# Coupled rotations of a hybrid layer: a twisted first layer and elementwise cycles in place of a first layer per cycle

## The chip, the cores and the metric

The kernel runs on one core of one Trainium2 chip. The core has five engines that work side by side, each in its own program order: TensorE (PE in the profile; PEld are its weight loads), VectorE (DVE), ScalarE (ACT), GpSimd (POOL) and SyncE (SP), whose queue issues nearly all DMAs here. The metric is the device time of one launch in microseconds.

## The reference, cut to what matters

`x` is 2 x 2048 tokens of 256 features, all float32. Four residual steps follow each other: a grouped softmax attention ("attention A"), the coupled rotation ("ffn"), a causal linear attention with rotary keys ("attention B"), and the coupled rotation again with the same weights. The change lies in the two rotations. Their input is the layer-normalized `x`:

```python
def _twist(x):
    o_r, o_i, p_r, p_i = jnp.split(x, 4, axis=-1)
    return jnp.concatenate([p_r, -p_i, -o_r, o_i], axis=-1)
gf = _global_net(x.mean(axis=1, keepdims=True), ...)    # one number a batch
out = x
for _ in range(3):
    tf = _coupling_net(out, ...)   # 256 -> 256 -> 128 -> 64 -> 1, gelu between, sigmoid last
    coupling = 0.1 + adaptive_range * (0.7 * gf + 0.3 * tf - 0.5) * 2.0
    out = out + coupling * _twist(out)
```

Each token has one coupling a cycle. Twisting twice gives the negative of the input.

## The kernel before, in words

The tokens `xs` stay in SBUF as 32 tiles of 128 tokens x 256 features; they form NB = 8 blocks of BLK = 512 tokens (four a batch). For matrix work a block is normalized and turned by PE into `zq`, [128 features, 2 halves, 512 tokens]. Attention A fills three quarters of the time and is not touched. Everything after it is in `behind`.

`rotations` builds one rotation as a set of small functions. Its unit is k = 0 to 11: pair of blocks k % 4 (two blocks, e = 0 and 1), cycle k // 4. `first(k, e)` is the first layer of one block (L817: two halves of the result, each two products over 128 features; the profile counts two matmuls for each, 8 a call) and its Gelu on ACT (L818). `second(k)` (L827), `third(k)` (L839, both blocks in one bank) and `fourth(k)` follow. In the first two cycles `fourth` makes the coupling of each token on all 128 partitions (L852, tanh on ACT L857, scaling on DVE L858) and updates `zq` in place: one half on DVE (L861, L863), the other on POOL (L862, L864). In the third cycle `back` takes over: the coupling comes out by tokens from eight tiny products (L891), `turn_back` turns `zq` back to tokens on PE (L875) and DVE adds it to `xs` (L879), then adds the twisted part times the coupling (L912). In the second rotation each half block is then stored (L918).

The order of the work is written out by hand: the calls at the end of `behind` follow one another, and `in_order` binds PE, DVE, ACT and POOL to that order. `rounds(f, n)` gives the steady part of a rotation: on even n the fourth layer of k - 2 (third cycle), the second of k - 1 and a first, on odd n the third of k - 1, the fourth of k - 2 and the other first. All matmul results share a ring of seven PSUM banks (`bank`); tiles of SBUF come from small rings by tag (`take`). `context(b)` is the global net in four steps. `Block` is one block of attention B: `look` and `norm` (statistics, normalization; `norm` also adds a constant to `xs` on POOL, L1017), `turn`, `query`, `key` (`rotated`: products on POOL L1034 and L1037, shuffles on DVE, sums in `rotate` L1047), `values`, `narrow`, `gates`, `keys_by_tokens`, `energies`, `learn`, `output`, `project_out`, `add_out`, and `next_look`, `next_norm`, `next_turn` for the second rotation's input. The loop over blocks runs block j beside the projections of block j + 1; the first rotation ends in the preparation of block 0, and the second one begins inside block 7. `statistics` (L106 to L111) has a power on POOL. L119 is the product of the two normalizing numbers of a token tile.

## Time and profile before

| | |
|---|---|
| time, median of 3 runs | 2101.61 us (2099.9 to 2102.15) |
| profiled execution | span 2096.9 us from first to last instruction; its whole time is not listed beside it |
| attention A | until about 1505 us |
| first rotation, then preparation of block 0 | 1505 to 1692 us |
| attention B, blocks 0 to 7 | 1692 to 1943 us |
| rest of the second rotation | 1943 to 2097 us |
| first layer L817 | 384 matmuls, 176.1 us |
| turning back L875 | 128 matmuls, 15.8 us |
| update on POOL, L862 and L864 | 32 + 32, mean 1769 and 1777 ns |
| scaling on DVE, L858 | 32, mean 1023 ns |

In a row of a group, the line and engine come first, then the tile written and the tiles read with shapes and count, then the busy time, the mean of one and the idle time before them with what ended it. A table of stretches gives, for each stretch, its length, the busy time and count of PE, PEld, DVE, ACT and POOL, then the granted clock of TensorE as a share of full speed, the DMA engines' busy share and GB/s. The chain in order of time names the work that ended last, with start and length. Matmuls overlap, so their mean times add up to more than PE's busy time.

### The profile page before, as it was taken

The page shows a single profiled execution, that of the slowest core. Times are in us where ns is not written, and L with a number is a line of the kernel's source. Part 1 is how long each engine was busy: PE and PEld are TensorE (multiplying, and loading weights), DVE is VectorE, ACT ScalarE, POOL GpSimd, SP SyncE. Part 2 cuts the span into 40 slices and gives each one's busy share as a digit, 9 for nine tenths or more (in the row PEclk, how much of TensorE's full clock was granted, in tenths as well). Part 3 has the DMA queues.
Part 4 walks back from the last instruction along what each step waited for, and adds up shares of the span by engine and source line. Part 5 has one row for each costly group of instructions (what it writes and reads, how often), then busy time and mean ns, then how long its engine had stood idle before and what let it go on. Part 6 is the DMA issues. An engine that isn't in the chain of part 4 may idle for free.

```text
span 2096.9 us, 38755 instructions
## 1 busy us (share of the span) xinstructions
PE 2079.2 (99%) x14158; PEld 1009.5 (48%) x14158; DVE 1699.3 (81%) x3241; ACT 1427.6 (68%) x2787; POOL 355.8 (17%) x352
## 2 busy tenths in 40 slices
PE   9999999999999999999999999999999999999998
PEld 4444444444444444444444444444444567776434
DVE  7899989998998999999899899988134688886336
ACT  4477777777777777777777777778864445554443
POOL 3100010000001000000000000000135355542451
PEclk9999999999999999999999999999999999999999
DMA  6511010110101011010110101100100000000002
GB/s 200 149 45 40 18 38 17 50 30 27 38 18 47 10 47 40 17 48 10 47 39 19 38 19 49 38 20 8 53 1 1 0 2 1 1 2 2 0 0 81
DMA packets 59696, 68.72 MB, mean 33 GB/s; under 512 B 24944, under 2 KB 34032, under 8 KB 59248
## 3 DMA queue, kind: packets, MB, share of 16 engines
q1 hardware_dynamic: 58592, 64.79, 11.2%
q8 instruction: 111, 1.82, 0.3%
q10 hardware_dynamic: 720, 0.92, 0.2%
q14 instruction: 81, 0.66, 0.1%
q0 software_dynamic: 192, 0.52, 0.1%
HBM read 35.78 MB, written 26.21 MB: 30 GB/s over the span
## 4 chain that ended last, share of the span: by engine, by line
PE 96%; DVE 2%; ACT 1%; DMA 1%; issue 0%; POOL 0%; SPq 0%; DVEq 0%; ACTq 0%; POOLq 0%
PE av L632 24%; PE s L376 24%; PE p L650 11%; PE q1f L817 8%; PE p L654 6%; PE q2f L827 4%; PE pe L1126 2%; PE bpo L1152 2%; PE pv L984 1%; PE po L499 1%; PE pq L975 1%; PE pk L975 1%; PE pw L984 1%; PE q3f L839 1%; PE pq L336 1%; DVE mx L380 1%
## 5 line engine op out<-in xcount | busy, mean ns | idle before, releaser
L380 DVE TENSOR_REDUCE mx<-s 128x1 f32<-128x512 f32 x2048 | 1273.8, 683 | 103.6 <-PE s L376 97.7
L658 ACT ACTIVATE e<-p 128x512 f32<-128x512 f32 x2048 | 1057.7, 602 | 306.3 <-PE p L654 299.5
L376 PE MATMUL s<-a_kP,qP 64*128 64x512 f32 x2048 | 707.3, 470 | 4.4 <-DVE mx L380 2.4
L654 PE MATMUL p<-a_m,a_pick 64*128 64x512 f32 x2048 | 578.0, 414 | 0.0
L376 PEld LDWEIGHTS s<-a_kP,qP 64*128 64x128 f32 x2048 | 283.6, 184 | 568.9 <-DVE mx L380 533.3
L632 PE MATMUL av<-e,a_v 128*32 128x512 f32 x4096 | 546.2, 605 | 0.1
L650 PE MATMUL p<-qP,a_kP 64*128 64x512 f32 x2048 | 521.8, 394 | 2.0 <-ACT e L658 2.0
L650 PEld LDWEIGHTS p<-qP,a_kP 64*128 64x128 f32 x2048 | 283.4, 185 | 65.4 <-issue 15.9
L654 PEld LDWEIGHTS p<-a_m,a_pick 64*128 64x128 f32 x2048 | 282.0, 184 | 24.0
L817 PE MATMUL q1f<-zq,wf 128*128 128x512 f32 x384 | 176.1, 601 | 0.0
L632 PEld LDWEIGHTS av<-e,a_v 128*32 128x32 f32 x4096 | 80.9, 108 | 128.1 <-issue 119.1
L398 POOL TENSOR_TENSOR mt<-nm,mt 128x16 f32<-128x16 f32 x31 | 6.9, 222 | 742.9 <-ACT mt L397 742.9
L818 ACT ACTIVATE a1f<-q1f,wf 128x512 f32<-128x512 f32 x96 | 65.8, 687 | 94.5 <-PE q1f L817 91.3
L817 PEld LDWEIGHTS q1f<-zq,wf 128*128 128x128 f32 x384 | 70.2, 190 | 96.9 <-issue 86.2
L1132 DVE TENSOR_TENSOR en<-pe,small 128x512 f32<-128x512 f32 x128 | 79.4, 683 | 11.8 <-PE pe L1126 11.8
L858 DVE TENSOR_SCALAR cf<-cf,f_beta,alphaf 128x512 f32<-128x512 f32 x32 | 32.7, 1023 | 67.6 <-ACT cf L857 67.6
L827 PE MATMUL q2f<-a1f,wf 128*128 128x512 f32 x192 | 87.0, 595 | 0.0
L237 POOL TENSOR_TENSOR ql<-zq,qh 128x512 f32<-128x512 f32 x15 | 19.4, 1292 | 364.5 <-ACT qh L234 364.5
L862 POOL TENSOR_TENSOR tf<-cf,zq 128x512 f32<-128x512 f32 x32 | 56.6, 1769 | 102.3 <-DVE cf L858 101.8
L829 ACT ACTIVATE a2f<-q2f,wf 128x512 f32<-128x512 f32 x48 | 32.7, 686 | 56.2 <-PE q2f L827 56.2
L864 POOL TENSOR_TENSOR zq<-zq,tf 128x512 f32<-128x512 f32 x32 | 56.9, 1777 | 2.5
L491 POOL TENSOR_TENSOR oc<-oc,sums 128x512 f32<-128x512 f32 x16 | 20.6, 1289 | 210.2 <-DMA sums<-dr 126.8
(210 smaller groups left out, 1634.6 us busy)
## 6 DMA issues: line engine op xcount, KB each, us to landing
qP<-dq SPq DMA_DIRECT2D x64, 256.0 KB
dq<-qh SPq DMA_DIRECT2D x62, 128.0 KB
dq<-ql SPq DMA_DIRECT2D x62, 128.0 KB
a_kP<-dk SPq DMA_DIRECT2D x16, 256.0 KB
oc<-avs SPq DMA_DIRECT2D x128, 32.0 KB
sums<-dr SPq DMA_DIRECT2D x128, 32.0 KB
out<-xs SPq DMA_DIRECT2D x16, 256.0 KB
xs<-in_x SPq DMA_DIRECT2D x7, 512.0 KB
```

The lines of the kernel that those rows point to most:

```text
L376: mm(s, qP[r // 2][row, qi * P : (qi + 1) * P], kP[r // 2][row, k0 + kb * BLK : k0 + (kb + 1) * BLK], start=True, stop=True,)
L380: nc.vector.tensor_reduce(mx[:, r, qi : qi + 1, kb], s, AX.X, ALU.max)
L632: mm(av[32 * r : 32 * r + 32, :], vA[:, units[u][0] // BPB * KB + kb, 32 * r : 32 * r + 32], es[r], start=(kb == 0), stop=(kb == KB - 1),)
L650: mm(t[r], kP[r // 2][row, k0 : k0 + P], qP[r // 2][row, :], start=True, stop=False)
L654: mm(t[r], pick[row, :], mrow[r // 2][row, :], start=False, stop=True)
L658: nc.scalar.activation(es[r], t[r], AF.Exp, scale=1.0 / HD**0.5)
L817: mm(q1, w1[:, c, m * P : (m + 1) * P], z[:, c, :], start=(c == 0), stop=(c == 1))
L818: nc.scalar.activation(a1[:, m, :], q1, AF.Gelu, bias=b1[:, m : m + 1])
L827: mm(q2, w2[:, c, :], a1[:, c, :], start=(c == 0), stop=(c == 1))
L862: nc.gpsimd.tensor_tensor(t1, cs, z[:, 0, :], ALU.mult)
L864: nc.gpsimd.tensor_tensor(z[:, 1, :], z[:, 1, :], t1, ALU.subtract)
L1132: nc.vector.tensor_tensor(self.ens[t][w], pes[w].rearrange("p (h n) -> p h n", h=4), const("triu").unsqueeze(1).to_broadcast([P, 4, P]), A ...
```

## The change

With u the first layer of z (without bias) and v the first layer of the twisted z, the first layer after a cycle with coupling c1 is u + c1 v, and that of the twisted result is v - c1 u. So `first` now keeps u (a copy out of PSUM, by DVE, or by ACT in block 7), `twist` makes v with a second set of weights `twisted` and writes it over z in `zq`, and `couple` forms the next cycle's first layer elementwise: in cycle 1 h = u + c v on DVE and v - c u on POOL, in cycle 2 h + c v with one of the two products on POOL. `again` applies bias and Gelu to it out of SBUF. The first layer is made twice per block instead of three times, and `back`, `turn_back` and `turn_ahead` go.

The tokens are now updated from `x` itself: each token's result is a combination of its normalized features and their twist with two numbers from the three couplings. The couplings of cycles 1 and 2 exist along the free axis; one partition's row of each goes to DRAM and comes back by tokens (`rows`, two DMAs a cycle and block and one back a pair, on SP). `ready` and `weigh` (`weights_of`) form the numbers, and `apply` does four token tiles: two scalings of twisted halves (POOL, or ACT in two places) and one step on DVE. The normalizing numbers are kept for all blocks (`scales0`, `scales1`). Pairs are staggered: `period(f, p, aside)` runs pair p through cycle 1, pair p - 1 through cycles 2 and 3, and the update of pair p - 2. In block 0 of attention B the query's and key's first product moves from POOL to DVE.

```diff
-beta = hold.tile([P, 1], F32, name="f_beta")
-nc.vector.tensor_scalar(beta, plain, sign, None, ALU.mult)
+
+twisted = hold.tile([P, 2, D], F32, name="f_twisted")
+for c in range(2):
+    nc.vector.tensor_scalar(twisted[:, c, :], w1[:, 1 - c, :], sign, None, ALU.mult)
+nc.vector.tensor_scalar(twisted[:, 0, :], twisted[:, 0, :], -1.0, None, ALU.mult)
+scales1 = hold.tile([P, 2, NB, 4], F32, name="scales1")
...
+    def activate(k, cycle, e, of, tags=(("qs", "ks"), ("rotq", "rotk"))):
+        a1 = acts[k, e] = take(tags[min(cycle, 2) - 1][e], [P, 2, BLK], f"a1f{n}_{k}_{cycle}_{e}")
         for m in range(2):
+            nc.scalar.activation(a1[:, m, :], of(m), AF.Gelu, bias=b1[:, m : m + 1])
+    def layer(w, k, e, name, between=()):
+        z = blk(zq, 2 * k + e)
+        q = [bank(f"{name}{n}_{k}_{e}_{m}") for m in range(2)]
+        for m in range(2):
+            if m == 1:
+                for step in between:
+                    step()
             for c in range(2):
+                mm(q[m], w[:, c, m * P : (m + 1) * P], z[:, c, :], start=(c == 0), stop=(c == 1))
+        return q
+    def first(k, e, copy=nc.vector.tensor_copy):
+        q = layer(w1, k, e, "q1f")
+        activate(k, 1, e, lambda m: q[m])
+        straight[k, e] = take(("gate", "v")[e], [P, 2, BLK], f"uf{n}_{k}_{e}")
+        for m in range(2):
+            copy(straight[k, e][:, m, :], q[m])
+    def twist(k, e, between=(), copy=nc.scalar.copy):
+        q = layer(twisted, k, e, "q5f", between)
+        for m in range(2):
+            copy(blk(zq, 2 * k + e)[:, m, :], q[m])
+    def second(k, cycle, e):
+        a1 = acts.pop((k, e))
+        q2 = bank(f"q2f{n}_{k}_{cycle}_{e}")
+        for c in range(2):
+            mm(q2, w2[:, c, :], a1[:, c, :], start=(c == 0), stop=(c == 1))
+        narrow[k, e] = take("en", [P, BLK], f"a2f{n}_{k}_{cycle}_{e}")
+        nc.scalar.activation(narrow[k, e], q2, AF.Gelu, bias=b2)
+    def third(k, cycle):
+        q3 = bank(f"q3f{n}_{k}_{cycle}")
         for e in range(2):
+            mm(q3[64 * e : 64 * e + 64, :], w3, narrow.pop((k, e)), start=True, stop=True)
+        narrow[k] = take("en", [P, BLK], f"a3f{n}_{k}_{cycle}")
+        nc.scalar.activation(narrow[k], q3, AF.Gelu, bias=b3)
+    def fourth(k, cycle):
+        a3 = narrow.pop(k)
+        q4 = [bank(f"q4f{n}_{k}_{cycle}_{e}") for e in range(2)]
         for e in range(2):
             row = slice(64 * e, 64 * e + 64)
             mm(q4[e], w4[row, :], a3[row, :], start=True, stop=True)
         for e in range(2):
+            c = turns[k, e] = take("en", [P, BLK], f"cf{n}_{k}_{cycle}_{e}")
+            nc.scalar.activation(c, q4[e], AF.Tanh, bias=hb4, scale=0.5)
+    def couple(k, cycle, e, tags=("kt", "kt2"), own_tags=("rotq", "rotk"), spare=nc.gpsimd):
+        c = turns.pop((k, e))
+        nc.vector.scalar_tensor_tensor(
+            c, c, plain, plains[2 * k // BPB].to_broadcast([P, BLK]), ALU.mult, ALU.add
+        )
+        if (k, 1) not in rows:
+            rows[k, 1] = dram.tile([4, BLK], F32, tag="cr", name=f"cr{n}_{k}")
+        at = 2 * (cycle - 1) + e
+        nc.sync.dma_start(rows[k, 1][at : at + 1, :], c[0:1, :])
+        v = blk(zq, 2 * k + e)
+        if cycle == 1:
+            u, h = straight[k, e], take(tags[e], [P, 2, BLK], f"hf{n}_{k}_{e}")
+            sums[k, e] = h
+            back = [take("qeo", [P, BLK], f"tf{n}_{k}_{e}_{m}") for m in range(2)]
+            for m in range(2):
+                nc.vector.tensor_tensor(h[:, m, :], c, v[:, m, :], ALU.mult)
+                nc.vector.tensor_tensor(h[:, m, :], h[:, m, :], u[:, m, :], ALU.add)
+                spare.tensor_tensor(back[m], c, u[:, m, :], ALU.mult)
+            for m in range(2):
+                spare.tensor_tensor(v[:, m, :], v[:, m, :], back[m], ALU.subtract)
+        else:
+            h = acts[k, e] = take(own_tags[e], [P, 2, BLK], f"a1f{n}_{k}_{cycle}_{e}")
+            u = sums.pop((k, e))
+            spare.tensor_tensor(h[:, 1, :], c, v[:, 1, :], ALU.mult)
+            nc.vector.tensor_tensor(h[:, 0, :], c, v[:, 0, :], ALU.mult)
+            for m in range(2):
+                nc.vector.tensor_tensor(h[:, m, :], h[:, m, :], u[:, m, :], ALU.add)
+        if (cycle, e) == (2, 1):
+            rows[k] = hold.tile([P, 2, 8], F32, name=f"ct{n}_{k}")
+            nc.sync.dma_start(
+                rows[k].rearrange("p c t -> p (c t)"),
+                rows[k, 1].rearrange("c (t p) -> p (c t)", p=P),
+            )
+    def again(k, cycle, e, tags=("rotq", "rotk")):
+        if cycle == 2:
+            activate(k, cycle, e, lambda m: sums[k, e][:, m, :], ((), tags))
+        else:
+            h = acts[k, e]
+            for m in range(2):
+                nc.scalar.activation(h[:, m, :], h[:, m, :], AF.Gelu, bias=b1[:, m : m + 1])
+    def ready(k):
+        c, f = rows.pop(k), take("small", [P, 2, 8], f"ab{n}_{k}")
+        nc.vector.tensor_tensor(f[:, 0, :], c[:, 0, :], c[:, 1, :], ALU.mult)
+        nc.vector.tensor_scalar(f[:, 0, :], f[:, 0, :], -1.0, 1.0, ALU.mult, ALU.add)
+        nc.vector.tensor_tensor(f[:, 1, :], c[:, 0, :], c[:, 1, :], ALU.add)
+        quarter[k] = f
+    def weights_of(k):
+        a3, f = narrow.pop(k), quarter.pop(k)
+        q4 = bank(f"q4f{n}_{k}_3")
         for tile in range(4):
             mm(
                 q4[:, 2 * tile : 2 * tile + 2], a3[:, tile * P : (tile + 1) * P], w4_pair,
                 start=True, stop=True,
             )
+        c, g = (take("small", [P, 2, 8], f"{a}f{n}_{k}") for a in ("c", "g"))
+        nc.scalar.activation(
+            c[:, 0, :].rearrange("p (e t) -> p e t", e=2), q4[:, 0:8].rearrange("p (t e) -> p e t", e=2),
+            AF.Tanh, bias=hb4, scale=0.5,
+        )
+        nc.vector.tensor_scalar(c[:, 0, :], c[:, 0, :], plain, plains[2 * k // BPB], ALU.mult, ALU.add)
+        nc.vector.tensor_tensor(g, f, c[:, 0:1, :].to_broadcast([P, 2, 8]), ALU.mult)
+        nc.vector.tensor_tensor(c[:, 0, :], f[:, 0, :], g[:, 1, :], ALU.subtract)
+        nc.vector.tensor_tensor(c[:, 1, :], f[:, 1, :], g[:, 0, :], ALU.add)
+        sc = scaled[:, :, 2 * k : 2 * k + 2, :].rearrange("p s e t -> p s (e t)")
+        by_rs, by_nb = take("small", [P, 3, 8], f"r{n}_{k}"), take("small", [P, 2, 8], f"n{n}_{k}")
+        nc.vector.tensor_tensor(by_rs[:, 0:2, :], c, sc[:, 0:1, :].to_broadcast([P, 2, 8]), ALU.mult)
+        nc.vector.tensor_tensor(by_nb, c, sc[:, 1:2, :].to_broadcast([P, 2, 8]), ALU.mult)
+        nc.vector.tensor_scalar(by_rs[:, 2, :], by_rs[:, 1, :], -1.0, None, ALU.mult)
+        nc.vector.tensor_scalar(by_rs[:, 0, :], by_rs[:, 0, :], 1.0, None, ALU.add)
+        nc.vector.tensor_tensor(g[:, 0, :], by_nb[:, 0, :], by_nb[:, 1, :], ALU.add)
+        nc.vector.tensor_tensor(g[:, 1, :], by_nb[:, 0, :], by_nb[:, 1, :], ALU.subtract)
+        quarter[k] = by_rs, g
+    def apply(k, e, by_tile=(nc.gpsimd.tensor_scalar,), home=None):
+        by, of = quarter[k]
+        j = 2 * k + e
+        if home is not None:
+            others = take(home, [P, 4, D], f"of{n}_{j}")
+        for t in range(4):
+            i = 4 * e + t
+            x = xs[:, 4 * j + t, :]
+            other = take("swap", [P, D], f"of{n}_{j}_{t}") if home is None else others[:, t, :]
+            x4, o4 = (a.rearrange("p (u f) -> p u f", u=4) for a in (x, other))
+            for m, (to, frm) in enumerate((
+                (slice(0, 4, 3), slice(2, 0, -1)), (slice(1, 3), slice(3, None, -3)),
+            )):
+                by_tile[t % len(by_tile)](
+                    o4[:, to, :], x4[:, frm, :], by[:, 1 + m, i : i + 1], of[:, m, i : i + 1], ALU.mult, ALU.add,
+                )
+            nc.vector.scalar_tensor_tensor(x, x, by[:, 0, i : i + 1], other, ALU.mult, ALU.add)
+            if store and t % 2:
+                s0 = (j % BPB) * BLK + (t - 1) * P
+                nc.sync.dma_start(
+                    out[j // BPB, s0 : s0 + 2 * P, :].rearrange("(t p) d -> p t d", p=P),
+                    tokens(j)[:, t - 1 : t + 1, :],
+                )
+    return context, first, twist, second, third, fourth, couple, again, ready, weights_of, apply
...
-            nc.gpsimd.tensor_tensor(r[:, m, :], a[:, m, :], c, ALU.mult)
+            (nc.gpsimd if j else nc.vector).tensor_tensor(r[:, m, :], a[:, m, :], c, ALU.mult)
...
+def period(f, p, aside, early=False):
+    first, twist, second, third, fourth, couple, again, ready, weigh, apply = f[1:]
+    def beside(n):
+        for step in aside.get(n, ()):
+            step()
+    q, o = p - 1, p - 2
+    if not early:
+        first(p, 0)
+    beside(0)
+    if o >= 0:
+        weigh(o)
+    again(q, 2, 0)
+    if o >= 0:
+        apply(o, 0)
+    beside(1)
+    twist(p, 0)
+    again(q, 2, 1)
+    for e in range(2):
+        second(q, 2, e)
+    beside(2)
+    first(p, 1)
+    if o >= 0:
+        apply(o, 1)
+    beside(3)
+    third(q, 2)
+    twist(p, 1, (step(fourth, q, 2), step(couple, q, 2, 0)))
+    beside(4)
+    second(p, 1, 0)
+    couple(q, 2, 1)
+    again(q, 3, 0)
+    second(p, 1, 1)
+    beside(5)
+    second(q, 3, 0)
+    again(q, 3, 1)
+    third(p, 1)
+    beside(6)
+    second(q, 3, 1)
+    beside(7)
+    fourth(p, 1)
+    couple(p, 1, 0)
+    beside(8)
+    third(q, 3)
+    ready(q)
+    couple(p, 1, 1)
+    beside(9)
...
 # the order of calls in the first rotation after pair 0's cycle 1 (one call a line in the code):
+period(f, 1, {2: (step(turn_next, 6), step(norm, 7)), 6: (step(turn_next, 7),), 7: (step(next, front1),), ...}, True)
+period(f, 2, {5: (step(next, more),), 8: (step(next, more),)})
+period(f, 3, {1: (zero.look,), 4: (step(zero.norm, late),), 6: (zero.turn, one.look)})
+zero.query(); one.norm(work); weigh(2); zero.rotate(); zero.key(); again(3, 2, 0, ...); again(3, 2, 1, ...)
+zero.values(0); second(3, 2, 0); second(3, 2, 1); zero.rotate(); zero.narrow(); third(3, 2); one.turn()
+fourth(3, 2); couple(3, 2, 0, ...); zero.values(1); couple(3, 2, 1, ...); zero.gates(); zero.keys_by_tokens()
+zero.halve(0); again(3, 3, 0); again(3, 3, 1); second(3, 3, 0); zero.ready(0); zero.energies(0)
+second(3, 3, 1); zero.learn(0); third(3, 3); ready(3)
 # in block 0 of attention B: weigh0(3), then apply of pairs 2 and 3 with the scalings on ACT
...
 # after block 7, the second rotation:
+period(f, 1, {0: (x.next_turn,), 3: (step(next, front1),), 4: ..., 6: ..., 8: ...}); period(f, 2, {})
 first(3, 0)
+weigh(1); again(2, 2, 0); apply(1, 0); twist(3, 0); again(2, 2, 1)
 first(3, 1)
+apply(1, 1); second(2, 2, 0); second(2, 2, 1); twist(3, 1, (step(third, 2, 2),)); fourth(2, 2); couple(2, 2, 0)
+second(3, 1, 0); second(3, 1, 1); couple(2, 2, 1); third(3, 1); again(2, 3, 0); again(2, 3, 1); fourth(3, 1)
+couple(3, 1, 0); second(2, 3, 0); second(2, 3, 1); couple(3, 1, 1); third(2, 3); again(3, 2, 0); again(3, 2, 1)
+second(3, 2, 0); ready(2); second(3, 2, 1); weigh(2); third(3, 2); fourth(3, 2); couple(3, 2, 0); couple(3, 2, 1)
+apply(2, 0); again(3, 3, 0); again(3, 3, 1); second(3, 3, 0); second(3, 3, 1); apply(2, 1); third(3, 3)
+ready(3); weigh(3); apply(3, 0, (by_act, nc.gpsimd.tensor_scalar)); apply(3, 1, (by_act, nc.gpsimd.tensor_scalar))
```

## The prediction

> **What bounds the kernel now.** I read the page first (busy shares, slices, chain), then the table of stretches, then the chain in order of time through a rotation, then the timeline of VectorE (DVE) and GpSimd (POOL).
>
> ```profile
> PE 2079.2 (99%) x14158; PEld 1009.5 (48%) x14158; DVE 1699.3 (81%) x3241; ACT 1427.6 (68%) x2787; POOL 355.8 (17%) x352
> PE 96%; DVE 2%; ACT 1%; DMA 1%; issue 0%; POOL 0%; SPq 0%; DVEq 0%; ACTq 0%; POOLq 0%
> ```
> ```profile
> 1740.00:1760.00 20.00, 20.00 (x216) 15.62 (x220) 15.70 (x44) 10.33 (x24) 8.68 (x12) 1.00 0.00 1
> ...
> 2000.00:2020.00 20.00, 20.00 (x53) 7.76 (x52) 7.44 (x9) 9.07 (x14) 11.68 (x7) 1.00 0.00 0
> ```
> ```profile
> 1995.89 3.63 PE q1f L817 x8
> 1999.52 3.43 PE q2f L827 x8
> 2002.95 3.43 PE q1f L817 x8
> 2007.39 1.06 PE q4f L852 x4
> 2008.45 3.63 PE q1f L817 x8
> ```
> The columns of a stretch after its length are PE, weight loads, DVE, ACT, POOL. TensorE (PE) is full in both rotations; in a rotation DVE is idle 63% of the time, in the attention between them (first line) only 22%. One cycle of one pair of blocks takes 12.57 us (1995.89 to 2008.45), all PE: two first layers (3.63 + 3.43), a second (3.43), a third (1.02, left out of the merged chain) and a fourth (1.06). The third cycle replaces the fourth layer's 1.06 by eight tiny matmuls (0.97) and 16 transposes (1.81). A pair costs 2 x 12.57 + 14.3 = 39.5 us.
>
> What the change will meet stands in the timeline (start, us, engine, line):
> ```profile
> 1997.36 0.69 DVE L861 TENSOR_TENSOR tf<-cf,zq 128x512 f32<-128x512 f32 x1
> ...
> 1999.83 1.50 DVE L858 TENSOR_SCALAR cf<-cf,f_beta,alphaf 128x512 f32<-128x512 f32 x1
> ```
> ```profile
> 1997.40 1.78 POOL L862 TENSOR_TENSOR tf<-cf,zq 128x512 f32<-128x512 f32 x1 [4.96 <-DVE cf L858]
> 1999.26 1.78 POOL L864 TENSOR_TENSOR zq<-zq,tf 128x512 f32<-128x512 f32 x1
> ```
> ```profile
> L1047 DVE TENSOR_TENSOR rotq<-rotq,swapqs x12: 682/685/1762, 1700.7 to 1859.9; 128x512 f32<-128x512 f32 x12
> ```
> POOL's 128x512 product takes 1.78 us when it starts 0.04 us behind a DVE product with both inputs in SBUF, 1.27 elsewhere (L1034): it stood 0.5 us until DVE was done. The DVE scaling at 1999.83, issued behind POOL's, takes 1.50 where 0.55 is usual. L1047 has a median of 685 ns and a maximum of 1762. So such instructions of the two engines exclude each other; their times add.
>
> **What is removed.** L817 has 384 matmuls, 8 a call, 48 calls; after it are 32 (a straight and a twisted call per block): 16 x 3.53 = 56.5 us. The transposes: 8 x 1.81 = 14.5. Together 71 us of PE, all on the path. A pair needs 4 x 3.53 + 3 x 3.43 + 3 x 1.02 + 2 x 1.06 + 0.97 = 30.6 us.
>
> **What is added, per pair.** DVE: four copies of 0.6 from PSUM; 18 products and sums of 128x512 with two SBUF inputs at 0.60 back to back (10 in cycle 1, 8 in cycle 2) = 10.8; eight `apply` steps of 128x256 (0.42 by L1157, 0.38 back to back) = 3.0; 13 tiny operations, 2.0. POOL: eight products and differences in cycle 1, two in cycle 2, at 1.24 back to back = 12.4; 16 scalings of 128x128 with two scalars, a form not in the trace: between 0.20 (a 4-element product, L119) and 0.73 (128x256 product, L1017), and I take 0.35, nearer the tiny one for half the elements and one tensor input = 5.6. ACT: four copies of 0.59 from PSUM, and the Gelus as before; some 20 us, no bound. The two-SBUF-input work and POOL's add to 10.8 + 3.0 + 12.4 + 5.6 = 31.8 us, over PE's 30.6: a second bound at once, before any latency.
>
> Whether the `apply` forms exclude each other too, no row shows. The Trainium skill ("SBUF — State Buffer", Who interferes with whom) says that a VectorE instruction with two SBUF inputs and a GpSimd instruction reading SBUF hold one port pair in turn, the later fully blocked. That would cover them; if they overlapped, the sum would be some 3 us a pair lower.
>
> **One period** (`period`, t = 0 where PE begins the fourth layer of a pair's cycle 1). From 1594.63 (q4f) to 1596.65 (L858) DVE gets the coupling after 2.0 us. `couple` of both blocks: ten DVE steps of 0.6, 0.4 for `ready`, and since each next DVE step finds a POOL product already waiting, seven of 1.24 between: 15.1, so the last sum stands at 17.1. Gelu 0.7, last half of the second layer 0.9: 18.7. PE had work for 10.7 of that (fourth 1.06, third 1.02, next pair's first 3.43, 0.97, twist 3.43, and the other second layer until it too waits). Then first, third, half a twist: the next fourth at 24.9, its coupling at 27.0. DVE meanwhile: copies 1.2, tiny 1.6, `apply` 8 x 0.35 + 4 x 0.38 = 4.3, copies 1.2, second `apply` 2.9 (POOL is ahead): 28.3. `couple` of cycle 2: eight steps and two POOL products, 7.3: 35.6; Gelu and half a second layer: **37.2 us**, against 30.6 of PE and 39.5 before. 6.7 of the 8.9 gained come back as waits.
>
> **The sum**, waits of PE that today has none:
> - opening to the first fourth layer (six first-layer calls, four turns and small work in the same stretch): 2.5.
> - rotation 0: period 1 carries two turns and the context, 3.7; period 2, 5.3 (the linear weights' DVE work hides in its slack); period 3 has `zero.look` (DVE 1.9) ahead of `apply`, `zero.norm` (four POOL sums of 0.73 between the two cycle-2 products) and the 1.1 of the offset: 43 us, 11.5 of it waiting.
> - pair 3's cycles 2 and 3 beside block 0's query, key and values (28 us of PE): `couple` to 17.1, then DVE and POOL in order through the query's rotation, `weigh`, `rotate` and the key's before `couple` starts at 32, ends at 39.4, and third layer and energies end at 42.7: 14.5.
> - block 0 of the attention takes 16 `apply` steps (6 us DVE, 32 ACT scalings) into a stretch with 22% of DVE free: 3 (0 to 6).
> - rotation 1: period 1, 4; period 2, 6.7.
> - the end, from pair 2's fourth layer, with no other work to fill: pair 2's coupling at 27.6, pair 3's at 37.0, its last sum 51.8, its cycle 2 coupling 58.5, sums 65.8, last third layer 69.2, `apply` of pair 2 until 73.2, `ready` and `weigh` 75.3, eight `apply` steps 80, output 3 more (2093.8 to 2096.9 today): 83 us for 51 of work that today follows without waits: 31.6. The coupling rows go out by SP and return in 4-byte pieces; a round trip's rows: 1.6 us (rs from ds) a hop, the mean packet 64 engine-ns (11.2% of 16 spans over 58592) times 2048 over 16 queues = 8.2. Between 3 and 11 us against 10.5 free: hidden.
>
> Waits 82.8, less 71: plus 11.8. Last, the clock:
> ```profile
> 2085.00:2090.00 5.00, 3.05 (x21) 1.92 (x19) 3.80 (x14) 1.64 (x3) 0.00 (x0) 0.94 0.20 69
> 2090.00:2097.00 7.00, 0.00 (x0) 0.00 (x0) 3.80 (x15) 0.00 (x0) 0.00 (x0) 0.50 0.45 152
> ```
> The granted clock (third column from the right) is 0.50 once PE stands idle, and PE would stand 4 to 8 us at a time at the end. Halved matmuls there cost between nothing and the 6 us of PE work on that chain; I take half, 3. Rows cannot price it in the periods. The skill ("TensorE: Matmul & The Clock Gate", Part 1) wants 3.4 us idle for the fall and 3.4 us busy for the return; each of five stalls would then cost up to 1.7 us more, and the sum would be about 8 higher, partly behind DVE.
>
> Span 2096.9 + 11.8 + 3 = 2111.7; the median shown, 2101.6, lies 4.7 above the span (start and stop around it, the own time of that execution not being listed), so **2116 us**. Its own bounds: POOL's scaling at 0.20 or 0.73 (-10, +15 where it is on the path, some five periods' halves and the end), block 0 and clock (3 each way): 2100 to 2134.
>
> **Rivals.**
> A, faster: POOL's products fall into DVE's gaps instead of between its steps, so the last sum of cycle 1 stands by 11 us, before PE runs out of work. It decides at that point: then periods are 31 to 32 and waits fall by some 5 in five periods and 10 more at handover and end, 2116 - 35 = 2081. For it: in today's cycle POOL is only 58% busy and DVE 37%. Against: the 1.78 and 1.50 rows.
> B, much slower: POOL's scaling near its upper bound and the clock falling in every stall: 2116 + 15 + 10 = 2141.
> C: the returned coupling rows land after 10.5 us and `ready` holds DVE, with both blocks' `couple` queued behind it: plus 2 in each of six places, 2128.
> That the matmuls do not go is no case: the order of instructions has 9501 PE rows for 9565, and 32 first-layer calls.
>
> **How the numbers follow.** Forecast 0.50, A 0.31, B 0.12, C 0.07. The range must reach A and most of B: 2078 to 2140; the forecast's own is 2100 to 2134. Some 0.2% (4 us) can be told from no change: 2097.4 to 2105.8 is the same. Faster: A and little else, 0.32; same: the low edge of the forecast, 0.08; slower 0.60.
>
> **What would show it.** PE under 90% in the rotations with waits on a1 (ACT, behind DVE's sums) before the second layer; DVE sums in `couple` of 1.8 us beside POOL's 1.24; periods of 37 us; a tail of some 80 us behind pair 2. Wrong if the 128x512 sums have a median of 0.69 with POOL at 1.27, periods come to 31, or POOL's scaling takes over 0.5.

## The result, and the profile after

The changed kernel takes 2137.5 us (median of 4 runs, 2135.8 to 2139.8) against 2100.8 for the kernel before on the same chip: a ratio of 1.0178 (95% interval 1.0164 to 1.0193). It is slower by 36.8 us; the forecast was slower by 14.4. The profiled execution spans 2136.9 us, 40.0 more than the one before. (Each run takes 1.8 us longer than its span, so the span before, 2096.9, belongs to a run of some 2098.7, a short one; that is why 40.0 is more than 36.8.) The page's busy times, then the chain's shares:

```profile
PE 2047.9 (96%) x13902; PEld 981.0 (46%) x13902; DVE 1795.8 (84%) x3279; ACT 1461.3 (68%) x2865; POOL 420.5 (20%) x452
...
PE 84%; DVE 10%; ACT 2%; POOL 2%; issue 1%; DMA 1%; SPq 0%; POOLq 0%; DVEq 0%; ACTq 0%
```

PE's idle time (span less busy) is 89.0 us where it was 17.7, and DVE's part of the chain has gone from 2% to 10%. PE's busy time fell by only 31.3 us, although 71 us of its work were to go; some of the products that stay take longer (a matmul of the second layer, L847, 688 ns instead of 595), in part because of the clock, as will be shown. The stretches (PE, weight loads, DVE, ACT, POOL, then granted clock) in attention B, in the second rotation and at the end:

```profile
1740.00:1760.00 20.00, 20.00 (x183) 13.26 (x182) 17.22 (x46) 9.36 (x22) 11.75 (x12) 1.00 0.01 2
2015.00:2035.00 20.00, 16.02 (x41) 6.75 (x40) 17.15 (x31) 8.22 (x14) 17.48 (x19) 0.91 0.04 13
2100.00:2120.00 20.00, 14.26 (x30) 4.98 (x28) 10.24 (x22) 6.84 (x11) 7.92 (x10) 0.60 0.08 11
```

In the rotation PE is no longer full. DVE and POOL are busy 17 of 20 us each, and much of that is waiting, as the groups show (busy, mean ns of one):

```profile
L888 POOL TENSOR_TENSOR tf<-cf,uf 128x512 f32<-128x512 f32 x32 | 54.5, 1722 | 44.2 <-DVE cf L873 43.5 <-ACT zq L841 0.7
...
L887 DVE TENSOR_TENSOR hf<-hf,uf 128x512 f32<-128x512 f32 x32 | 52.4, 1637 | 1.1
...
L886 DVE TENSOR_TENSOR hf<-cf,zq 128x512 f32<-128x512 f32 x32 | 39.1, 1222 | 0.6
```

A sum of 0.6 us (0.69 alone) takes 1.64, and POOL's product 1.72 instead of 1.27: each stands until the other engine's step is done (e1 and e2 test this). One period of the chain in order of time:

```profile
1577.37 1.11 PE q4f L865 x4
...
1588.52 1.64 DVE hf L887
1590.15 1.69 DVE hf L886
...
1591.87 1.64 DVE hf L887
...
1594.30 2.08 PE q2f L847 x2
...
1614.91 1.11 PE q4f L865 x4
```

The last sum of cycle 1 ends 16.1 us behind the start of the fourth layer (1577.4 to 1593.5; forecast 17.1), then PE's second layer follows, at half its speed (2.08 us for two matmuls that take 1.12), and the next fourth layer starts 37.5 us behind the first.

The table cuts the profiled executions at matmuls that both rotations and all versions have. P1 to P3: from the fourth layer (cycle 1) of pair 0 to those of pairs 1, 2 and 3 in the first rotation. H: from there to the query of block 1. B: to the second rotation's first layer. S: to the fourth layer of pair 1. P5: to that of pair 2. E: to the end. All in us; the start of P1 differs by up to 3 us between executions (1537.6 to 1540.9), so stretches are compared rather than spans.

| version | P1 | P2 | P3 | H | B | S | P5 | E | median (us) |
|---|---|---|---|---|---|---|---|---|---|
| changed kernel | 39.4 | 37.5 | 42.5 | 46.6 | 229.0 | 77.8 | 37.5 | 88.7 | 2137.5 |
| e1 couple on DVE | 35.9 | 34.8 | 43.4 | 42.4 | 228.8 | 74.0 | 35.9 | 76.8 | 2111.8 |
| e2 POOL writes only | 29.9 | 33.2 | 36.4 | 39.5 | 228.9 | 68.9 | 31.4 | 73.8 | 2084.2 |
| e3 apply on DVE | 38.7 | 38.2 | 42.2 | 45.9 | 228.8 | 77.7 | 38.3 | 88.6 | 2142.1 |
| e4 PE kept busy | 37.1 | 37.6 | 42.5 | 47.0 | 229.1 | 75.9 | 37.3 | 88.7 | 2139.6 |
| e5 second buffer | 39.6 | 37.6 | 42.5 | 46.6 | 227.0 | 78.9 | 37.7 | 88.7 | 2138.4 |
| e6 keys later | 38.7 | 37.6 | 43.0 | 43.3 | 227.6 | 77.8 | 37.5 | 88.7 | 2135.8 |
| e7 order at two joints | 39.5 | 37.6 | 42.5 | 46.5 | 229.1 | 70.7 | 37.7 | 86.3 | 2130.6 |
| e8 DVE, deferred | 29.9 | 33.8 | 42.8 | 42.6 | 228.9 | 68.9 | 35.1 | 72.5 | 2095.9 |
| e9 updates spread | 39.8 | 37.7 | 42.5 | 46.6 | 225.7 | 77.9 | 37.5 | 88.6 | 2136.1 |
| e10 e8 and joints | 29.9 | 33.8 | 41.8 | 40.7 | 225.7 | 67.9 | 33.8 | 75.7 | 2088.9 |
| e11 and mixed scalings | 29.9 | 43.4 | 43.7 | 39.4 | 225.7 | 67.9 | 43.3 | 81.6 | 2115.3 |
| e12 and earlier look | 29.9 | 42.3 | 45.8 | 39.5 | 225.7 | 67.9 | 43.3 | 81.6 | 2116.1 |
| e13 updates at block ends | 39.9 | 37.7 | 42.5 | 46.6 | 221.6 | 78.2 | 37.7 | 88.7 | 2132.0 |
| e14 the best | 29.9 | 33.8 | 41.8 | 40.7 | 221.6 | 67.9 | 33.8 | 72.6 | 2082.2 |

The kernel before has only some of these cuts: B is 219.9 there; from its first first layer (1504.9) to block 1's query it takes 187.2 us (changed kernel 199.1), from the second rotation's first layer to the end 185.0 (204.0). So of the 40.0, 11.9 are lost in the first rotation with the handover, 9.1 in attention B and 19.0 in the second rotation.

### The profile page after: what moved, and what is told of

Read it like the earlier page. It is cut to its first block, busy times and chain, and to the rows that moved or that the text cites. A ratio compares the mean times of both kernels' runs of the same rounds, so it can differ in the third digit from the quotient of the medians.

```text
span 2136.9 us, 38472 instructions
## 1 busy us (share of the span) xinstructions
PE 2047.9 (96%) x13902; PEld 981.0 (46%) x13902; DVE 1795.8 (84%) x3279; ACT 1461.3 (68%) x2865; POOL 420.5 (20%) x452
## 4 chain that ended last, share of the span: by engine, by line
PE 84%; DVE 10%; ACT 2%; POOL 2%; issue 1%; DMA 1%; SPq 0%; POOLq 0%; DVEq 0%; ACTq 0%
PE av L633 23%; PE s L378 23%; PE p L651 11%; PE p L655 6%; DVE hf L887 2%; PE q2f L847 2%; DVE hf L886 2%; PE pe L1178 2%; PE q1f L826 2%; PE bpo L1204 1%; PE q5f L826 1%; PE po L500 1%; PE pw L1036 1%; PE pv L1036 1%; PE pq L1027 1%; PE pk L1027 1%
## 5 line engine op out<-in xcount | busy, mean ns | idle before, releaser
L847 PE MATMUL q2f<-a1f,wf 128*128 128x512 f32 x192 | 107.6, 688 | 47.2 <-ACT a1f L815 32.7
L847 PEld LDWEIGHTS q2f<-a1f,wf 128*128 128x128 f32 x192 | 36.0, 207 | 107.4 <-ACT a1f L815 51.6
L888 POOL TENSOR_TENSOR tf<-cf,uf 128x512 f32<-128x512 f32 x32 | 54.5, 1722 | 44.2 <-DVE cf L873 43.5
L826 PE MATMUL q1f<-zq,wf 128*128 128x512 f32 x128 | 62.2, 631 | 0.0
L826 PE MATMUL q5f<-zq,f_twisted 128*128 128x512 f32 x128 | 60.4, 607 | 0.0
L849 ACT ACTIVATE a2f<-q2f,wf 128x512 f32<-128x512 f32 x48 | 32.7, 684 | 37.1 <-PE q2f L847 30.8
L967 DVE SCALAR_TENSOR_TENSOR xs<-xs,r,of 128x256 f32<-128x256 f32 x64 | 32.9, 530 | 26.2 <-POOL of L964 22.5
```

Of the source, the lines that this page charges most:

```text
L826: mm(q[m], w[:, c, m * P : (m + 1) * P], z[:, c, :], start=(c == 0), stop=(c == 1))
L847: mm(q2, w2[:, c, :], a1[:, c, :], start=(c == 0), stop=(c == 1))
L888: spare.tensor_tensor(back[m], c, u[:, m, :], ALU.mult)
```

## The experiments

**e1: couple on DVE alone.**

```diff
-def couple(..., own_tags=("rotq", "rotk"), spare=nc.gpsimd):
+def couple(..., own_tags=("rotq", "rotk"), spare=nc.vector):
```

> Edit: couple's products and differences on POOL move to DVE (spare=nc.vector); all else as in the changed kernel. Theory (two-input DVE and POOL instructions take turns): the sums of cycle 1 (hf L887) fall from 1.64 to 0.69 us, the last sum of a pair's cycle 1 stands 11 to 12 us after its fourth layer instead of 16, periods of 33 to 34 us instead of 37.5, and the time falls from 2137 to about 2112 (2104 to 2120). Rival 1 (DVE's load and its chain of steps set the period): DVE gets 20 more steps of 0.6 us in two pairs, 6 us a pair, and the time rises to 2150 or more. Rival 2 (the lowered clock after waits is most of the loss): 2125 to 2135.

2111.8 us, ratio to before 1.0047 (1.0032 to 1.0062). Ten products and differences a pair more on DVE, and it is 26 us faster. The sum is back at its own length:

```profile
L887 DVE TENSOR_TENSOR hf<-hf,uf 128x512 f32<-128x512 f32 x32 | 22.1, 692 | 1.1
```

**e2: POOL writes where it read.** Left out: the difference v - c u of cycle 1; POOL writes zeros instead, twenty times a pair.

```diff
     nc.vector.tensor_tensor(h[:, m, :], h[:, m, :], u[:, m, :], ALU.add)
-    spare.tensor_tensor(back[m], c, u[:, m, :], ALU.mult)
-for m in range(2):
-    spare.tensor_tensor(v[:, m, :], v[:, m, :], back[m], ALU.subtract)
+    for _ in range(5):
+        spare.memset(back[m], 0.0)
```

> Leaves out part of the computation: v - c u of cycle 1 isn't made; POOL's four instructions there are replaced by ten memsets (write only) of the same scratch tiles, about 5 us of POOL a block as before. Theory as the trace shows it (turns are taken only where POOL reads SBUF too, as in the products): DVE's sums at 0.69 beside a busy POOL, last sum 8 to 9 us after the fourth layer, periods of 31 to 33, time about 2105 (2095 to 2115). If any POOL work holds DVE up, its sums stay over 1 us and the time stays above 2125. Rival 1 (DVE's own chain): no change, 2130 to 2140.

2084.2 us, ratio 0.9913 (0.9896 to 0.993), lower than expected. POOL stays as busy beside the sums (20 memsets of 0.53 us a pair for eight products and differences, forecast at 1.24), but reads nothing:

```profile
L889 POOL MEMSET tf<- 128x512 f32 x160 | 83.7, 531 | 7.4
L887 DVE TENSOR_TENSOR hf<-hf,uf 128x512 f32<-128x512 f32 x32 | 22.1, 692 | 1.1
```

So it is POOL's reading of SBUF beside DVE's two inputs that costs, not POOL being busy. The rule of the Trainium skill that the prediction cites ("SBUF — State Buffer", Who interferes with whom) names just this condition, and these rows agree with it: 692 ns beside writes, 1637 beside reads. The rest of e2's gain over e1 (P1 29.9 to 35.9) is, by its size, DVE's eight steps of the difference, which nobody makes here; e8, where they come later, has the same P1.

**e3: apply's scalings on DVE**, the rival that POOL's 0.54 us each were the missing cost.

```diff
-def apply(k, e, by_tile=(nc.gpsimd.tensor_scalar,), home=None):
+def apply(k, e, by_tile=(nc.vector.tensor_scalar,), home=None):
```

> Edit: apply's scalings of 128x128 on DVE instead of POOL (except in block 0 and for the last pair, where ACT takes them or half of them). Theory: in a period DVE is free for cycle 2 only 0.3 us after the coupling arrives, so a period loses less than 0.5 us; the end, where 16 POOL scalings of 0.52 stand on the chain (9.6 us), gets some 4 us shorter: 2131 (2126 to 2136). Rival (POOL's scaling at 0.54 instead of the 0.35 that was predicted is the missing cost): 8 tiles x 0.35 us a pair come back in every period, 2115 to 2122.

2142.1 us, ratio 1.019 (1.0175 to 1.0205): a little slower, above both ranges. Two scalings on DVE take 2 x 0.34 and then the step; from POOL DVE waits about as long for them. P2 is 38.2 against 37.5. The 4 us expected at the end did not come either: E is 88.6 against 88.7, because DVE now has the scalings and the steps one after the other, 1.04 us a tile where POOL and DVE together took 1.11.

**e4: PE kept busy in its wait.** Five extra products with constants (ten rows of the profile) ahead of one second layer a period.

```diff
+for _ in range(warm):
+    mm(q2, w2[:, 0, :], twisted.rearrange("p c d -> p (c d)"), start=True, stop=True)
```

> Adds five matmuls of a constant (128x512, into the bank that the second layer overwrites) where PE waits for block 1's cycle-2 Gelu in each period: nothing of the result changes. Rival 2 (clock): granted clock back to 1.00 in those stretches, the second layer after the wait 1.1 instead of 2.1 us and the next first layer 3.6 instead of 4.2: 1.5 us in each of five periods, 2130 (2126 to 2133). Theory (DVE's turns set the period, DVE is free only 0.3 us after the coupling): most of that is lost in DVE's wait, under 0.5 us a period, 2134 to 2138.

2139.6 us, ratio 1.0175 (1.016 to 1.019): no gain. In the first periods of the two rotations the stretches P1 and S are 2 us shorter each, in the steady ones nothing moves (37.6, 37.3), although the first layer behind the wait runs at full speed again (3.60 us instead of 4.20). But in P2 the extra products also end 0.9 us behind the Gelu that PE waits for, which uses up what the clock gives back: the next fourth layer (cycle 2) starts 26.0 us behind the first, against 25.9. So there e4 by itself does not price the clock. The rows of the changed kernel do:

```profile
1604.38 1.27 ACT L868 ACTIVATE cf<-q4f,f_hb 128x512 f32<-128x512 f32 x2 [2.24 <-PE q4f L865]
1604.90 0.48 DVE L967 SCALAR_TENSOR_TENSOR xs<-xs,r,of 128x256 f32<-128x256 f32 x1 [0.35 <-POOL of L964]
1605.31 0.75 DVE L873 SCALAR_TENSOR_TENSOR cf<-cf,f_plain,plainf 128x512 f32<-128x512 f32 x1
```

The first of the two tanh ends at 1605.07, and DVE is done with its `apply` steps at 1605.31, so an earlier coupling could have been taken up only 0.2 us sooner.

**e5: a second buffer for the updates in block 0.**

```diff
-apply0(3, 0, home="zt")
+apply0(3, 0, home="kt2")
```

> In block 0 of attention B the update of pair 3's first block puts its scaled halves into another tile (kt2) than the update before it (zt); all else is as in the changed kernel. In the changed kernel ACT's scalings for that block wait 2.74 us for DVE to read the tile, the gate's tanh stands behind them in ACT's order, and PE waits 3.26 us for it, with eight products at half clock behind (3.78 instead of 1.99). Theory (the loss in block 0 is ACT's order): the tanh starts 2.5 to 2.9 us earlier, PE's wait falls under 1 us, the time falls by 3 to 5 us, to some 2133. Rival (it is DVE's load by the added steps, as the prediction had it): DVE's steps are the same and in the same order, so nothing over 1 us changes: 2137.

2138.4 us: no gain in time, and 2.0 us in B, about half of what was expected. PE's wait for ACT, first row (changed kernel), gives way to one for DVE, second row (e5):

```profile
1727.64 2.07 PE L1178 MATMUL pe<-qeo,rotk 32*128 32x256 f32 x10 [3.26 <-ACT gate L1140]
```
```profile
1733.19 1.11 PE L1048 MATMUL pt<-small,rotk 128*128 128x128 f32 x4 [2.54 <-DVE og L1209]
```

Neither theory holds: both engines are late here, one just behind the other.

**e6: keys turned later at the handover.**

```diff
 zero.gates()
-zero.keys_by_tokens()
 zero.halve(0)
+zero.ready(0)
+zero.energies(0)
 again(3, 3, 0)
 again(3, 3, 1)
 second(3, 3, 0)
-zero.ready(0)
-zero.energies(0)
 second(3, 3, 1)
+zero.keys_by_tokens()
 zero.learn(0)
```

> Between the rotations the keys of block 0 are turned to tokens (keys_by_tokens) behind pair 3's third cycle instead of ahead of it, and block 0's first energies ahead of it. In the changed kernel ACT's copies of the turned keys wait 7.04 us for the tile that still holds pair 3's sums, until DVE has made the last of them, and the Gelus of pair 3's third cycle stand behind them in ACT's order. Theory: the Gelus start by about 1691 instead of 1693.96, PE's wait of 4.5 us falls to about 2, the query of block 1 starts 2 to 4 us earlier (1703.9 now): time 2134, between 2133 and 2136. Rival (DVE's sums alone set that end, the second block's at 1695.7): the second block's Gelu and everything behind it stay where they are, less than 1 us: 2137.

2135.8 us, within the expected range; H falls from 46.6 to 43.3. In the changed kernel the copy of the turned keys stands on ACT ahead of pair 3's Gelus:

```profile
1692.19 1.07 ACT L1147 COPY kt<-pt 128x512 f32<-128x512 f32 x2 [7.04 <-DVE a1f L897]
...
1693.96 2.55 ACT L912 ACTIVATE a1f<-a1f,wf 128x512 f32<-128x512 f32 x4
```

In e6 the first Gelu starts 3.2 us behind DVE's scaling of the coupling (1689.43 to 1692.60) instead of 5.6 (1688.34 to 1693.96) in the changed kernel.

**e7: order at two joints.**

```diff
 third(0, 1)
-x.next_norm()
 fourth(0, 1)
+x.next_norm()
...
 third(3, 2)
+apply(2, 0)
 fourth(3, 2)
 couple(3, 2, 0)
 couple(3, 2, 1)
-apply(2, 0)
```

> Two places of the order are changed, far apart in time. Start of the second rotation: the fourth layer of pair 0 is issued ahead of the normalization of block 7, so that on ACT the tanh of the couplings is not behind four scalings that wait for block 7's statistics (tanh at 1973.9, 5.4 us behind the fourth layer, elsewhere 1.2). The end: the update of pair 2's first block is issued ahead of pair 3's last fourth layer instead of behind its sums, into 4 us in which DVE and POOL stand idle. Theory: the first period of the rotation shrinks by 3.5 to 4.5 us (42.2 to about 38, as the next one), the end by 2 to 3: 2131. Rival: the period is bounded by DVE and POOL in turn and not by its beginning, so that the first gain is given back by the next couplings: 2135.

2130.6 us, ratio 1.014 (1.0125 to 1.0155). S falls by 7.1 (expected 3.5 to 4.5), E by 2.4. In the changed kernel the tanh of the first couplings waits on ACT behind the scalings of block 7:

```profile
1971.94 2.08 ACT L126 ACTIVATE zt<-xs,scales 128x256 f32<-128x256 f32 x4 [3.46 <-POOL scales L121]
1973.93 1.24 ACT L868 ACTIVATE cf<-q4f,f_hb 128x512 f32<-128x512 f32 x2
```

In e7 the tanh follows 1.2 us behind the fourth layer instead of 5.4. The rest of the 7.1 is, as an estimate, the clock: in the changed kernel it is granted at 0.50 from 1983.08 to 1993.32, with 6.05 us of PE work that would take half as long at full speed, and in e7 it does not fall in this stretch.

**e8: couple on DVE, and v - c u behind the sums of both blocks.** `couple` only notes what it owes; `settle`, called in the next period behind `weigh` (and ahead of `zero.query` and behind the last `couple(3, 1, 1)`), makes it.

```diff
-    spare.tensor_tensor(back[m], c, u[:, m, :], ALU.mult)
-for m in range(2):
-    spare.tensor_tensor(v[:, m, :], v[:, m, :], back[m], ALU.subtract)
+owed.append((k, e, c, u, v))
```

> All of couple on DVE as in the experiment before (2111.8), and the two products and differences that make v - c u move behind the sums of both blocks, into the next period: no DVE step stands between the sums that PE waits for. Theory (the order of DVE's steps between fourth layer and last sum is what costs): the last sum stands 9 us after the fourth layer instead of 13 (with POOL 16), PE's work of 10.7 us covers it, periods of 32 to 33 us where DVE's other work lets them (34.8 and 35.9 with DVE alone, 37.5 in the changed kernel), the third one of the first rotation less (43.4, DVE full throughout): 2098, between 2092 and 2105. Rival (DVE's whole load of some 26 us a period with the gaps of POOL's scalings is the bound already): the sums come sooner but cycle 2's come no sooner, 2110.

2095.9 us, ratio 0.9974 (0.9965 to 0.9983): faster than before the change, by 0.26%. P1 falls to 29.9 and E by 16.1; P3 stays at 42.8, which the expectation had lower.

**e9: the four updates spread over blocks 0 to 3 of attention B**, in the middle of each.

```diff
 if j == 0:
     weigh0(3)
-    apply0(2, 0, home="zt")
+if j < 4:
+    apply0(2 + j // 2, j % 2, home="zt")
...
-if j == 0:
-    apply0(2, 1, home="zt")
-    apply0(3, 0, home="zt")
...
-if j == 0:
-    apply0(3, 1, home="zt")
```

> Against the changed kernel only block 0 of attention B is eased: of the four updates of block pairs 2 and 3 that stand in it (32 ACT scalings, 16 DVE steps), one stays and one goes into each of blocks 1, 2 and 3. In the changed kernel it takes 229.0 us from block 1's query to the second rotation's first layer, before the change 219.9; with a second buffer for the scalings it took 227.0, PE's wait for ACT giving way to one for DVE. Theory (block 0 alone has too much added to it on ACT and DVE, the other blocks have room): 221 to 223 us for that stretch, time 2130, between 2128.5 and 2132. Rival (attention B has no room for these steps anywhere, 22% of DVE idle is used by waits): the loss is spread like the steps, 2136.

2136.1 us, the rival's time; B is 225.7, between the two theories. Each update costs its block some 1.4 us.

**e10: e8 with the joints** (e6, e7, e9 in one).

> The version with couple on DVE and the differences deferred (2095.9) together with the three changes of order: keys turned later at the handover, updates spread over blocks 0 to 3, fourth layer ahead of the normalization at the start of the second rotation and pair 2's first update earlier at the end. Theory (the losses at the joints are waits of their own and add to that of the couplings): 2095.9 - 3 (handover) - 7 (block 0) - 4 (start) - 2 (end) = 2080, between 2076 and 2085. Rival (with couplings ready sooner the joints are covered, or DVE, now with all of couple, fills them): less than half of that, 2088 or more.

2088.9 us, ratio 0.996 (0.9946 to 0.9974). Less than the sum: against e8 P3 and S give 1.0 each, P5 1.3, H 1.9, B 3.2, and E loses 3.1.

**e11: ACT and POOL make the scalings in turn, on top of e10.**

```diff
-apply(o, 0)
+apply(o, 0, (by_act, nc.gpsimd.tensor_scalar))
```

> As the run before (joints), and in the periods the scalings of apply are made by ACT (0.40 us each) and POOL (0.54) in turn, so that DVE's eight steps a period follow at some 0.6 us instead of 1.1. Theory (with couple on DVE the waits of DVE for POOL's scalings are the next bound, above all in the third period of the first rotation, 42.8 us): 3 to 4 us off that period, 1 off others, 2075. Rival (ACT's scalings stand ahead of Gelus that PE waits for, or DVE is busy by its own work): no gain or a loss, 2080 to 2083.

2115.3 us, ratio 1.0081 (1.0066 to 1.0096): 26 us lost, much more than the rival had. P2 and P5 grow by 9.5 us, E by 5.9. The rows of ACT and PE in P2:

```profile
1588.28 0.88 ACT L1280 ACTIVATE of<-xs,gf,r 128x128 f32<-128x128 f32 x2 [4.59 <-DVE xs L974]
```
```profile
1590.78 3.78 PE L848 MATMUL q2f<-a1f,wf 128*128 128x512 f32 x4 [6.28 <-ACT a1f L816]
```

ACT's second pair of scalings waits for one of the two `swap` tiles, which DVE frees only behind the deferred differences; the Gelus of the sums stand behind it in ACT's order, and PE behind them. In e10, where POOL makes these scalings, PE has no such wait in P2.

**e12: block 0's statistics a period earlier, on top of e11.**

```diff
-period(f, 2, {5: (step(next, more),), 8: (step(next, more),)})
+period(f, 2, {5: (step(next, more),), 8: (step(next, more),), 9: (zero.look,)})
```

> As the run before (scalings by ACT and POOL in turn), and block 0's statistics for attention B (zero.look, 2.0 us of DVE) move from the third period of the first rotation, whose 42 us are DVE's, to the end of the second. Theory (the third period is DVE's own sum): 2 us less there, 1 more in the second: 2074, a gain of 1 to 2. Rival (the third period ends in POOL's offsets for block 0 standing between cycle 2's products and sums, or in ACT): same as the run before within 1.

2116.1 us: no gain; P3 is longer by 2.1 and P2 shorter by 1.1, the opposite of the theory. What holds P3 at 41.8 us or more in every version but e2 (36.4) is not settled by a run. The chain of e14 points at POOL's scalings, two pieces of it with 12 us together in P3, the first at half the pace of the second, while DVE makes the deferred differences (1614.64 to 1619.72):

```profile
1614.82 7.96 POOL of L971 x8
...
1626.45 4.10 POOL of L971 x8
```

**e13: the updates at the ends of blocks 0 to 3**, behind the last output, where DVE is idle.

```diff
 x.project_out(1)
+if j < 4:
+    apply0(2 + j // 2, j % 2, home="kt2" if j % 2 else "kt")
```

> Against the changed kernel the four updates of pairs 2 and 3 that stand in block 0 of attention B go into blocks 0 to 3, one each, at the end of the block, behind its last attention output and its projections, where DVE stands idle some 4 us of a block (spread in the middle of the blocks, each cost 1.4 us: 225.7 us from block 1's query to the second rotation's first layer; 229.0 in the changed kernel, 219.9 before). Theory (it is the place in the order of DVE and ACT that costs, not the load): 220 to 222 us, span 7 to 9 less than the changed kernel's. Rival (the load): 225 or more.

2132.0 us, ratio 1.0156 (1.014 to 1.0173); B is 221.6, 7.4 less than in the changed kernel. The same steps on the same engines cost 9.1 us in block 0, 5.9 in the middle of four blocks, 1.8 at their ends: it is where they stand, not the load. e13 also writes the scalings into other tiles (`kt` and `kt2` for `zt`), and no run separates that from the place.

**e14: the best version**: e8, e6, the first half of e7, and e13.

> The version with couple on DVE, the differences deferred, the keys turned later and the fourth layer ahead of the normalization (2088.9 with two further edits), with the updates at the ends of blocks 0 to 3 as in the run before and without the early update of pair 2. Theory (that early update delays the couplings now that DVE makes all of them: 75.7 us behind pair 2's fourth layer with it, 72.6 without; the place of the updates gives 4 to 5): 2081, between 2078 and 2084. Rival (the end is longer for another reason, or the updates cost by their load): 2086 or more.

2082.2 us (2081.0 to 2084.3), ratio 0.992 (0.9905 to 0.9935): 17 us faster than before the change and 55 faster than the change as made. E is 72.6 (e8: 72.5), so the early update of pair 2 is what cost e10 its 3.1 us.

## Why the prediction was right in direction and too low in size

**What held.** DVE's sums and POOL's products take turns; e1 and e2 show it from both sides. The steady period was forecast at 37.2 us and took 37.5 in both rotations, the third 43 and took 42.5. Its steps hold as well (P2, behind the fourth layer): the last sum stood at 16.1 (17.1), DVE was free for cycle 2 at 28.0 (28.3), and the last sum of cycle 2 stood at 35.4 (35.6). The prediction left open whether the `apply` steps and POOL's scalings exclude each other too. They do: a scaling takes 0.44 us alone and 0.69 when it starts behind one of DVE's steps, which have two inputs in SBUF as well (its mean is 541 ns, its median 448):

```profile
L964 POOL TENSOR_SCALAR of<-xs,r,gf x88: 442/448/1400, 1596.4 to 2132.8; 128x128 f32<-128x128 f32 x88
```

So one of the prediction's signs of being wrong, a scaling over 0.5 us, did come true in the mean, but by e3 it is not what made the kernel slower. The coupling rows (one row out a cycle and block, one transfer back a pair), rival C, hold nobody: DVE's `ready` (L917) starts without a wait. Rival A fails at its own point: the last sum stands at 16.1 us, not by 11. Rival B gave 2141, near the time, but not by its causes: the scaling is far from its upper bound of 0.73, cheaper ones on DVE gain nothing (e3), and the clock is worth some 4 us in the periods (e4). That 2137.5 lies within the wide range of 2078 to 2140 is therefore luck; it lies outside the forecast's own 2100 to 2134.

**The sum by its parts.** The step that failed is the sum of PE's waits: the mechanism is right, but its terms outside the steady periods are too small. The forecast's terms give the first rotation with the handover -35.5 + 37.5 = +2.0; attention B +3; the second rotation with the end -35.5 + 42.3 + 3 (clock) = +9.8. Measured: +11.9, +9.1, +19.0. Four terms make up most of what is missing:

- *Period 1 of a rotation, 3.7 and 4 us of waits.* The forecast gives no other cover for it than the steady period's 10.7 us of PE work behind the fourth layer. But the next pair's first layer has already been made in the first rotation, and only a twist remains:

```profile
1538.94 3.70 PE L826 MATMUL q5f<-zq,f_twisted 128*128 128x512 f32 x8
1543.78 1.12 PE L847 MATMUL q2f<-a1f,wf 128*128 128x512 f32 x2 [1.14 <-ACT a1f L815]
1547.13 2.07 PE L847 MATMUL q2f<-a1f,wf 128*128 128x512 f32 x2 [2.22 <-ACT a1f L815]
1551.20 2.08 PE L847 MATMUL q2f<-a1f,wf 128*128 128x512 f32 x2 [2.00 <-ACT a1f L815]
1554.55 2.08 PE L847 MATMUL q2f<-a1f,wf 128*128 128x512 f32 x2 [1.27 <-ACT a1f L815]
```

  The four waits add up to 6.6 us, and the products behind them lose some 4 more by the halved clock (2.07 for 1.12 three times, and the turn and first layer that follow): 11 instead of 3.7. e8, which leaves 9 us between fourth layer and last sum instead of 16, brings this period from 39.4 to 29.9.
- *The start of the second rotation*, in the same term of 4: a wait in ACT's order (tanh behind block 7's scalings, 5.4 us behind the fourth layer) that the forecast did not list. e7 gives 7.1 back. (e8, with this order unchanged, gives 8.9: with the sums ready sooner the late tanh costs little.)
- *The handover, 14.5.* 42.7 us were forecast from pair 3's fourth layer, 46.6 measured. Missed was a tile: the turned keys want `kt`, which still holds pair 3's sums, and ACT's Gelus stand behind that copy. e6 takes 3.3 of the 3.9 back.
- *Block 0, 3 (0 to 6).* Priced as DVE's load; it is where the steps stand in two engines' orders: 9.1, and 1.8 with place and tiles changed (e13).

At the end 83 + 3 was forecast from pair 2's fourth layer and 88.7 measured. Pair 2's sixteen scalings follow each other alone on the chain:

```profile
2115.05 9.57 POOL of L964 x16
```

The forecast let `apply` of pair 2 run from 69.2 to 73.2; it ran from 66.8 to 76.8, within a microsecond of the forecast's end once its 3 us of clock are added. What is left is the last eight steps, 7.0 us instead of 4.7, most of them waiting for scalings that wait for the tile before. Whether a scaling at the forecast's 0.35 us on POOL would shorten the end is not shown; making those of pair 2 on DVE at 0.34 does not (e3).

**The clock.** The forecast gave it 3 us at the end and none in the periods. PE's busy time came out 40 us above the work that was left. From 1546 us on the granted clock of the changed kernel is 0.50 in nine stretches with 52.9 us of PE work; at full speed that work would take about half, so by this estimate some 26 of the 40 are the clock's, and the rest is open. Two of the stretches, in P1 and at the end (length, PE, weight loads, DVE, ACT, POOL, clock):

```profile
1546.17:1559.82 13.65, 9.42 (x16) 4.11 (x17) 7.46 (x6) 6.53 (x13) 8.00 (x5) 0.50 0.00 0
2092.30:2116.20 23.90, 14.67 (x26) 4.96 (x25) 16.35 (x26) 6.83 (x11) 10.89 (x8) 0.50 0.02 1
```

How much of it was in the way is known for the periods only: e4 gains 2.3 us in P1 and 1.9 in S, and the median time does not show even these. At the handover, in block 0 and at the end the clock falls in e4 as before, and no run takes it away there, so the forecast's 3 us are neither shown nor refuted. The Trainium skill ("TensorE: Matmul & The Clock Gate", Part 1) wants some 3.4 us without work for the fall. In these traces less is enough at times, and not at others. In the rows of P1 two matmuls are at half speed behind a wait of 2.22 us, and in P2 again (the 2.08 at 1594.30, behind 2.22); behind the same 2.22 in S two take 1.13, full speed, as do four behind 1.71 (1.96, at 2065):

```profile
1981.93 1.13 PE L847 MATMUL q2f<-a1f,wf 128*128 128x512 f32 x2 [2.22 <-ACT a1f L815]
```

## What to carry to other kernels

Work taken from a full engine is worth only what its successors leave uncovered: before moving 128x512 arithmetic to two engines, count the two-input steps of DVE and the reading steps of POOL as one queue, and ask whether one engine alone, with the steps that nobody waits for put last, is not faster (2137.5 to 2095.9 here). Price the first and last round of a pipeline by their own cover, not by the steady one's. And read each added step's place in its engine's order, with the buffer it waits for: the same sixteen DVE steps and 32 scalings cost 9.1 or 1.8 us by their place and tiles, and scalings on ACT that wait for a tile cost 26.

## What the runs showed of the hardware

POOL's writes beside DVE cost DVE's sums nothing: 160 memsets of 0.53 us left them at 692 ns, reading products made them 1637. Even a product of 8 elements a partition (L917) took 1.23 us instead of 0.16 when POOL was reading. POOL's scaling of 128x128 with two scalars takes 0.44 us, 0.69 behind a DVE step with two inputs in SBUF, and on DVE 0.34 (e3's rows of L964). The granted clock fell to 0.50 behind waits of PE as short as 2.2 us.
